# Chosen experts and gates sent to the partitions of their LoRA rows through DRAM instead of by a TensorE product

## The chip, the cores and the metric

One core of one Trainium2 chip. The time is device microseconds of one execution of the whole kernel, the median of several runs. The profile is one further execution, recorded instruction by instruction.

## The reference

One layer on `x` of 128 batches, each 128 nodes by 1024 features, with an integer adjacency matrix for each batch. Cut to what matters:

```python
x = x + gnn(layernorm(x), adj, adj, W, a)          # Wh = h @ W, 16 heads of 64, masked softmax, att @ Wh, elu
y = layernorm(x)
logits = einsum('bh,eh->be', y[:, 0, :], router_w)  # E = 8 experts, from node 0 of the batch
top_vals, top_idx = top_k(logits, 2)                # two experts for each batch
gates = softmax(logits kept at top_idx, -inf elsewhere)
down = einsum('blh,erh->bler', y, lora_down)        # R = 16 rows an expert
x = x + y + einsum('bler,ehr,be->blh', down, lora_up, gates)
```

Each batch so has two chosen experts, of 16 LoRA rows each, and two gates.

## The kernel before

**Passes and gaps.** The batches are taken in 64 pairs, a pass q for each pair (and two passes to run out), and in 32 groups of four (G = 4). A pass of the loop at L835 loads the next pair and projects its own pair with W. The projection is done as seven products in the order 1, 6, 2, 5, 7, 3, 4 (`project`, L390 to 476), each 8 products of 128x128 by 260 columns in the program (L417) and 16 rows in the trace. Ahead of each product stands a list of tasks, a gap: gap 0 before product 1, gap 1 before product 6, gap 2 before product 2, gap 3 before product 5, gap 4 before product 7, gap 5 before product 3, gap 6 before product 4, and gap 7 after it. The order of every engine's instructions is the order in which the program writes them (`manual_schedule`, L71), so the gaps are an order written out by hand: an engine takes its instructions from the gaps one after the other and waits at each for its operands. SP, which issues most DMAs, is such a queue too. Waits between engines are set by the framework from the tiles' reads and writes.

**Where a group's experts are handled.** For group g:

- pass 2g+2, gap 6: `logits` (L609) makes the logits of four batches on PE, `choose` (L620) picks on DVE two experts a batch; `val[:, 0]` holds their numbers (as 8 - e) and `val[:, 1]` later the gates, a batch on each of 4 partitions.
- pass 2g+3, gap 0: `fetch` (L677) stands first, then `attention_weights` (L494) of another pair, then `weigh` (L657), which makes the gates.
- gap 3: `gates` (L696). Gap 4: `ffn_down` (L701), with `pd` (L707) on PE from the fetched rows of `down`, and ACT's multiplication by the gate (L713). Gaps 5 and 6: `ffn_up` (L715), from `up`.

The 128 LoRA rows of a group (4 batches, 2 slots, 16 rows) lie on 128 partitions. So the 8 experts' numbers have to come from 4 partitions to all 128 (`at_down`, L682, eight numbers on each partition, the addresses of eight gathers), and each number to the 16 partitions of its slot (`at_up`, L685, the addresses of one gather). The gates have to come to the partitions of their slot as well (`gate`, used in L713).

Before the change this is done by `spread` (L646) and `to_rows` (L667): DVE multiplies the two numbers of each batch by a row of the identity matrix, which gives 4 partitions by 8 numbers with zeros elsewhere; PE multiplies these by a matrix of ones (`ones_g`) and so puts all eight on every partition of a PSUM tile `pb`; DVE masks them with `slot` and sums, which gives the one number that belongs to each partition. `pb` takes a buffer of the pool `ps_m` (4 of them), as do `ph`, `pd`, `pu` and `pl`.

POOL issues the eight gathers of `down` (L688) and the one of `up` (L692). The last group has no `fetch`; it uses all experts densely.

**SP's queue** around it: in pass 2g+2 the load of `adj_i` (L105) in gap 5; ahead of gap 0 of pass 2g+3 two loads of `xt` (L101) and two of `xn` (L96); then the two transposes by DMA (L586) of gaps 2 and 3; then four stores (L730) in gap 6. `adj_f` (L107) is loaded through POOL's queue.

Of the kernel before, what the change touches and what calls it, by code (L numbers as in the profile page):

```python
# [8 lines left out]
F32 = mybir.dt.float32  # L9
# [5 lines left out]
ALU = mybir.AluOpType  # L15
AX = mybir.AxisListType
# [9 lines left out]
def adj_ffn_kernel(  # L26
# [15 lines left out]
    nc = tc.nc  # L42
    B, N, D = x.shape
    P = 128
# [6 lines left out]
    R = ER // E  # L51
    TOP = 2
    GR = TOP * R
    HALF = 512
# [3 lines left out]
    NG, _, G, _ = adj.shape  # L58
# [5 lines left out]
    const = ctx.enter_context(tc.tile_pool(name="const", bufs=1))  # L64
    work = ctx.enter_context(tc.tile_pool(name="work", bufs=2))
    small = ctx.enter_context(tc.tile_pool(name="small", bufs=3))
    ps_w = ctx.enter_context(tc.tile_pool(name="ps_w", bufs=2, space=bass.MemoryType.PSUM))
    ps_m = ctx.enter_context(tc.tile_pool(name="ps_m", bufs=4, space=bass.MemoryType.PSUM))
# [7 lines left out]
    GRP = {}  # L76


    dram = ctx.enter_context(tc.tile_pool(name="dram", bufs=1, space=bass.MemoryType.DRAM))
# [70 lines left out]
    ident = const.tile([P, P], F32, name="ident")  # L150
# [2 lines left out]
    nc.vector.memset(half_pow, -0.5)  # L153
    fold = small.tile([P, H], F32, tag="fold", name="fold", bufs=1)
    nc.vector.tensor_reduce(fold, ident.rearrange("p (t h) -> p h t", t=KH)[:, 0:H], AX.X, ALU.add)
    ones_g = const.tile([G, P], F32, name="ones_g")
    nc.vector.memset(ones_g, 1.0)

    order = const.tile([G, E], F32, name="order")
    for e in range(E):  # L160
# [118 lines left out]
        return fourths([router_sb[:, k] for k in range(KC)],  # L279
                       [down_sb.rearrange("p e r k -> p k (e r)")[:, k] for k in range(KC)])  # L280

    slot = down_row = up_row = None

    def experts(part):

        nonlocal slot, down_row, up_row
        pr = ps_m.tile([P, HALF], F32, tag="pm", name="pr")
        nc.tensor.matmul(pr[:, 0:E + ER], sum_of, part, start=True, stop=True)
        for t, lo, n in ((router_sb.rearrange("p k e -> p e k"), 0, E),
                         (down_sb.rearrange("p e r k -> p (e r) k"), E, ER)):  # L290
            nc.vector.tensor_tensor(t, t, pr[:, lo:lo + n, None].to_broadcast([P, n, KC]),
                                    ALU.subtract)
        nc.sync.dma_start(table.rearrange("(e p) c -> p e c", p=P),
                          down_sb.rearrange("p e r k -> p e (r k)"))

        slot = const.tile([P, 1, G * TOP], F32, name="slot")
        nc.vector.tensor_reduce(slot[:, 0], ident.rearrange("p (j r) -> p j r", r=R), AX.X,
                                ALU.add)
        rows = work.tile([P, P], I32, tag="hp", name="rows")
        nc.gpsimd.iota(rows, pattern=[[0, G * TOP], [1, R]], base=E * R, channel_multiplier=0)  # L300
        at_r = work.tile([P, P], F32, tag="hp", name="at_r")
        nc.vector.tensor_tensor(at_r, rows, ident, ALU.mult)
        up_row = const.tile([P, 1], F32, name="up_row")
        nc.vector.tensor_reduce(up_row, at_r, AX.X, ALU.add)
        row = small.tile([P, 1], I32, tag="row", name="row", bufs=1)
        nc.gpsimd.iota(row, pattern=[[0, 1]], base=E * P, channel_multiplier=1)
        down_row = const.tile([P, 1], F32, name="down_row")
        nc.vector.tensor_copy(down_row, row)
# [311 lines left out]
    def choose(g):  # L620

        st = GRP[g]
        both = small.tile([G, E + 1], F32, tag="lg", name="lg")
        nc.vector.tensor_copy(both, st["pl"][:G, 0:E + 1])
        lg, dev = both[:, 0:E], both[:, E:E + 1]
        top = small.tile([G, 8], F32, tag="top", name="top")
        nc.vector.max(out=top, in_=lg)

        val = small.tile([G, 2, TOP], F32, tag="val", name="val")
        first = small.tile([G, E], F32, tag="first", name="first")  # L630
        mark = small.tile([G, 2, E], F32, tag="mark", name="mark")
        for s in range(TOP):
            nc.vector.scalar_tensor_tensor(mark[:, s], lg, top[:, s:s + 1], order,
                                           op0=ALU.is_equal, op1=ALU.mult)
            if s:
                nc.vector.tensor_scalar(first, order, val[:, 0, 0:1], None, op0=ALU.is_equal)
                nc.vector.scalar_tensor_tensor(mark[:, s], first, float(-E), mark[:, s],
                                               op0=ALU.mult, op1=ALU.add)
            nc.vector.tensor_reduce(val[:, 0, s:s + 1], mark[:, s], AX.X, ALU.max)
        if g < NG - 1:  # L640
            st["experts"] = spread(val[:, 0], "experts")
        pr = small.tile([G, 2], F32, tag="pr", name="pr")
        nc.vector.tensor_sub(pr[:, 0:1], top[:, 1:2], top[:, 0:1])
        st.update(val=val, pr=pr, dev=dev)

    def spread(val, name):  # L646

        own = small.tile([G, G, TOP], F32, tag=name, name=name)
        nc.vector.tensor_tensor(own, ident[:G, :G, None].to_broadcast([G, G, TOP]),
                                val[:, None, :].to_broadcast([G, G, TOP]), ALU.mult)  # L650
        return own.rearrange("g t s -> g (t s)")

    def ratio(g):
        st = GRP[g]
# [2 lines left out]
    def weigh(g):  # L657

        st = GRP[g]
        gate, pr = st["val"][:, 1], st["pr"]  # L660
        nc.vector.tensor_scalar(gate[:, 0:1], pr[:, 1:2], 1.0, None, op0=ALU.add)
        nc.vector.reciprocal(gate[:, 0:1], gate[:, 0:1])
        nc.vector.tensor_mul(gate[:, 1:2], pr[:, 1:2], gate[:, 0:1])
        if g < NG - 1:
            st["gates"] = spread(gate, "gates")

    def to_rows(own, name):  # L667

        pb = ps_m.tile([P, HALF], F32, tag="pm", name="pb")
        nc.tensor.matmul(pb[:, 0:G * TOP], ones_g, own, start=True, stop=True)  # L670
        mine = small.tile([P, G * TOP], F32, tag="mine", name="mine")
        nc.vector.tensor_tensor(mine, pb[:, 0:G * TOP], slot[:, 0], ALU.mult)
        of_slot = small.tile([P, 1], F32, tag=name, name=name)
        nc.vector.tensor_reduce(of_slot, mine, AX.X, ALU.add)
        return pb, of_slot

    def fetch(g):  # L677

        st = GRP[g]
        pb, mine = to_rows(st["experts"], "of_slot")  # L680
        at_down = small.tile([P, G * TOP], U32, tag="at_down", name="at_down")
        nc.vector.tensor_scalar(at_down, pb[:, 0:G * TOP], float(-P), down_row, op0=ALU.mult,  # L682
                                op1=ALU.add)
        at_up = small.tile([P, 1], U32, tag="at_up", name="at_up")
        nc.vector.tensor_scalar(at_up, mine, float(-R), up_row, op0=ALU.mult, op1=ALU.add)  # L685
        st["down"] = work.tile([P, G * TOP * R, KC], F32, tag="down", name="down", bufs=1)
        for j in range(G * TOP):
            nc.gpsimd.indirect_dma_start(  # L688
                out=st["down"][:, j * R:(j + 1) * R].rearrange("p r k -> p (r k)"), out_offset=None, in_=table,
                in_offset=bass.IndirectOffsetOnAxis(ap=at_down[:, j:j + 1], axis=0))  # L690
        st["up"] = work.tile([P, D], F32, tag="up", name="up", bufs=1)
        nc.gpsimd.indirect_dma_start(  # L692
            out=st["up"], out_offset=None, in_=up_t,
            in_offset=bass.IndirectOffsetOnAxis(ap=at_up[:, 0:1], axis=0))

    def gates(g):  # L696

        st = GRP[g]
        st["gate"] = to_rows(st["gates"], "gate")[1]

    def ffn_down(g):  # L701

# [132 lines left out]
    for q in range(NQ + 2):  # L835
        gaps = [[] for _ in range(8)]
        if q == 0:
            prepare(gaps)
        g, part = divmod(q - 2, 2)
        ffn = 0 <= g < NG  # L840
        if ffn and not part:
            gaps[6] += [(logits, g), (choose, g)]
# [3 lines left out]
        if ffn and not part:  # L846
            gaps[6].append((ratio, g))
            if g == NG - 1:
                gaps[6] += [(down_dense, g, 3, 1), (weigh, g)]
# [27 lines left out]
        if ffn and part and g == NG - 1:  # L877
            gaps[0] += [(gates_dense, g), (up_dense, g)]
        elif ffn and part:
            gaps[0].insert(0, (fetch, g))  # L880
            gaps[0].append((weigh, g))
            gaps[3].insert(0, (gates, g))
            gaps[4].insert(0, (ffn_down, g))
            gaps[5].insert(0, (ffn_up, (g, 0)))
            gaps[6].append((ffn_up, (g, 1)))
# [14 lines left out]
        if q == 1:  # L900
            gaps[0].append((squares_of, 1))
            gaps[5].append(keep("tables", table_parts))
            gaps[7].append(keep("", experts, "tables"))
# [50 lines left out]
```

## Time and profile before

| what | value |
|---|---|
| median of 9 runs | 1948.74 us (1947.38 to 1949.59) |
| the profiled execution | 1948.96 us |
| its span, first to last instruction | 1947.2 us |
| granted TensorE clock, mean over the span | 0.996 of full speed |
| `down` gathers (L688), POOL | 248, 1015 ns each |
| `pw` (L417), PE, lhs xt / lhs s | 4080 and 3072 rows, 386 and 384 ns each |
| DMA traffic | 329.25 MB, 169 GB/s in the mean |

The page gives times in microseconds from the first instruction. PE are TensorE's matmuls, PEld its weight loads, DVE is VectorE, ACT ScalarE, POOL GpSimd, SP the engine that issues DMAs; a q behind a name is that engine's sequencer. "L707" is line 707 of the kernel. A row of the timeline has start, length, engine, line, operation, what is written from what, and, in brackets, how long the engine stood idle before it and what ended that. The mean duration of a matmul row holds the overlap with its neighbour; how long a stretch of PE's queue takes is better read from the chain of waits, where the pieces follow one another without overlap.

### The profile page before, as it was taken

To read this page: it belongs to the slowest core of one execution; us is meant where nothing else is said; L and a number is where in the kernel's file an instruction comes from. 1 tells how busy PE (TensorE), PEld (TensorE's weight loads), DVE (VectorE), ACT (ScalarE), POOL (GpSimd) and SP (SyncE) were. 2 spreads that over 40 slices of the span, in tenths; PEclk is the share of its full clock that TensorE was granted. 3 is DMA by queue.
4 is the path that set the end of the run, shared out by engine and by line. 5 is a ranking of instruction groups with operands and counts; after the bars stand their busy time and mean duration, and the time that the engine had idled before them with its cause. 6 is when DMAs were issued, how large, how long until landed. Compare 5 with 4: busy or idle time off the path is not lost.

```text
span 1947.2 us, 30291 instructions
## 1 busy us (share of the span) xinstructions
PE 1931.5 (99%) x11096; PEld 1574.7 (81%) x11096; DVE 1640.6 (84%) x3477; ACT 1088.1 (56%) x1060; POOL 833.8 (43%) x1135
## 2 busy tenths in 40 slices
PE   9999999999999999999999999999999999999997
PEld 6888888888888888888888888888888888888885
DVE  6888888888888888888888888888888888888886
ACT  3655556556555556555555555565555555555653
POOL 3345433355444355333454433553444553334540
PEclk9999999999999999999999999999999999999998
DMA  7455655665655656556546556556556565565452
GB/s 306 130 185 143 181 172 154 186 177 134 198 175 152 190 152 163 184 158 179 184 130 195 171 151 187 168 147 194 168 163 185 146 173 176 155 187 182 124 167 93
DMA packets 343955, 329.25 MB, mean 169 GB/s; under 512 B 274304, under 2 KB 276352, under 8 KB 343296
## 3 DMA queue, kind: packets, MB, share of 16 engines
q1 hardware_dynamic: 326080, 285.35, 49.9%
q0 software_dynamic: 17008, 40.91, 7.1%
q8 instruction: 88, 1.44, 0.3%
q10 hardware_dynamic: 720, 1.06, 0.1%
q14 instruction: 59, 0.48, 0.1%
HBM read 193.57 MB, written 67.63 MB: 134 GB/s over the span
## 4 chain that ended last, share of the span: by engine, by line
PE 95%; DVE 3%; ACT 1%; DMA 1%; issue 0%; POOL 0%; POOLq 0%; DVEq 0%; ACTq 0%
PE pw L417 79%; PE ph L534 6%; PE pu L723 3%; PE pd L707 3%; PE pb L670 1%; PE pl L614 1%; DMA tt<-halves 1%; PE pu L784 1%; DVE xn L553 0%; DVE hp L544 0%; DVE xn L552 0%; DVE stats L314 0%; ACT halves L584 0%; PE idle L149 0%; ACT y_t L590 0%
## 5 line engine op out<-in xcount | busy, mean ns | idle before, releaser
L417 PE MATMUL pw<-w_sb,xt 128*128 128x260 f32 (+1 forms) x4080 | 944.4, 386 | 0.0
L417 PEld LDWEIGHTS pw<-w_sb,xt 128*128 128x128 f32 x4080 | 764.7, 190 | 144.7 <-issue 27.5
L417 PE MATMUL pw<-w_sb,s 128*128 128x260 f32 (+1 forms) x3072 | 711.1, 384 | 1.9 <-DVE u L425 1.9
L417 PEld LDWEIGHTS pw<-w_sb,s 128*128 128x128 f32 x3072 | 578.1, 190 | 115.7 <-POOL xt L370 15.2
L318 POOL TENSOR_SCALAR rstd<-mv 128x2 f32<-128x2 f32 x126 | 27.6, 219 | 850.6 <-DVE mv L315 845.4
L590 ACT COPY y_t<-tt 128x2048 uint16<-128x2048 uint16 x126 | 313.3, 2505 | 68.8 <-DMA tt<-halves 68.4
L688 POOL DMA_INDIRECT down<-table,at_down x248 | 251.8, 1015 | 162.5 <-DVE e L508 88.8
L314 DVE BATCH_NORM_STATS2 stats<-xn 128x6 f32<-128x512 f32 x504 | 318.8, 674 | 0.1
L584 ACT COPY halves<-xn 128x2048 uint16<-128x2048 uint16 x126 | 239.5, 1901 | 124.6 <-DVE xn L553 79.7
L486 ACT ACTIVATE parts<-wh,rstd 128x512 fp32r<-128x512 f32 x192 | 134.2, 716 | 212.2 <-DVE wh L425 212.2
L551 ACT ACTIVATE ex<-hp 128x1024 f32<-128x1024 f32 x128 | 135.3, 1057 | 177.4 <-DVE hp L544 175.9
L727 DVE SCALAR_TENSOR_TENSOR xn<-pu,rstd,xn 128x512 f32<-128x512 f32 x248 | 169.0, 744 | 21.8 <-PE pu L723 21.8
L544 DVE TENSOR_TENSOR hp<-ph,att 128x512 f32<-128x512 f32 x256 | 161.3, 672 | 10.3 <-PE ph L534 10.0
L553 DVE SCALAR_TENSOR_TENSOR xn<-ex,xn 128x1024 f32<-128x1024 f32 x128 | 156.8, 1225 | 14.2 <-DVE xn L552 0.9
L534 PE MATMUL ph<-parts,adj_f 128*128 128x512 f32 x512 | 164.5, 443 | 1.3 <-ACT parts L486 0.8
L552 DVE SCALAR_TENSOR_TENSOR xn<-hp,xn 128x1024 f32<-128x1024 f32 x128 | 156.8, 1225 | 4.4
L425 DVE TENSOR_TENSOR wh<-pw,u 128x520 f32<-128x520 f32 (+1 forms) x128 | 89.2, 697 | 78.8 <-PE pw L417 75.4
L606 ACT ACTIVATE xn<-xn,off,mul 128x1024 f32<-128x1024 f32 x128 | 151.4, 1232 | 1.5 <-POOL off L571 1.5
L490 DVE SCALAR_TENSOR_TENSOR parts<-wh,rstd,parts 128x512 fp32r<-128x512 f32 x192 | 137.9, 746 | 11.1 <-ACT parts L486 11.1
L534 PEld LDWEIGHTS ph<-parts,adj_f 128*128 128x128 f32 x512 | 96.6, 189 | 20.9 <-ACT parts L486 1.2
L425 DVE TENSOR_TENSOR wh<-pw,p 128x520 f32<-128x520 f32 (+1 forms) x64 | 44.8, 699 | 81.3 <-PE pw L417 81.3
L319 POOL TENSOR_TENSOR rstd<-rstd,half_pow 128x2 f32<-128x2 f32 x126 | 89.9, 714 | 10.5
(156 smaller groups left out, 1486.3 us busy)
## 6 DMA issues: line engine op xcount, KB each, us to landing
xn<-in_x SPq DMA_DIRECT2D x128, 512.0 KB
xt<-in_x_t SPq DMA_DIRECT2D x127, 512.0 KB
out_y<-xn SPq DMA_DIRECT2D x124, 512.0 KB
adj_f<-in_adj_t POOLq DMA_DIRECT2D x32, 256.0 KB
adj_i<-in_adj SPq DMA_DIRECT2D x32, 256.0 KB
down<-table,at_down POOLq DMA_INDIRECT x248
w_sb<-in_w SPq DMA_DIRECT2D x3, 1040.0 KB
wt_sb<-in_w_t SPq DMA_DIRECT2D x1, 2048.0 KB
```

The costliest lines, as they stand in the source:

```text
L314: nc.vector.bn_stats(st[:, h, :], X[i][:, h * HALF:(h + 1) * HALF])
L417: nc.tensor.matmul(dst[:, j, cols], lhs[:, k, :], w_sb[:, rhs, k, j, cols], start=(first and k == 0), stop=(k == KH - 1), skip_group_check ...
L490: nc.vector.scalar_tensor_tensor(in_two(PARTS[q][:, 1, b]), block, rstd, in_two(PARTS[q][:, 0, b].bitcast(F32)), op0=ALU.mult, op1=ALU.sub ...
L534: nc.tensor.matmul(PH[i][h], GRP[g]["adj_f"][:, t, :], PARTS[q][:, s, NH * (i % 2) + h], start=(s == 0), stop=(s == 1))
L544: nc.vector.tensor_tensor(hp[:, h * HALF:(h + 1) * HALF].rearrange("p (h f) -> p h f", f=F), ph.rearrange("p (h f) -> p h f", f=F), att[:, ...
L552: nc.vector.scalar_tensor_tensor(xt, hp, 0.0, xt, op0=ALU.max, op1=ALU.add)
L553: nc.vector.scalar_tensor_tensor(xt, ex, 1.0, xt, op0=ALU.min, op1=ALU.add)
L584: nc.scalar.copy(halves, X[i].bitcast(U16).rearrange("p (d s) -> p s d", s=2))
L590: nc.scalar.copy(y_of(i).bitcast(U16).rearrange("p k (n s) -> p s k n", s=2), TT.pop(i).rearrange("p (s k) n -> p s k n", s=2))
L606: nc.scalar.activation(X[i], X[i], AF.Identity, bias=GRP[g]["off"][:, t:t + 1], scale=GRP[g]["mul"][:, t:t + 1])
L688: nc.gpsimd.indirect_dma_start(out=st["down"][:, j * R:(j + 1) * R].rearrange("p r k -> p (r k)"), out_offset=None, in_=table, in_offset=b ...
L727: nc.vector.scalar_tensor_tensor(y[:, cols], pu[t], st["rstd"][:, t:t + 1], y[:, cols], op0=ALU.mult, op1=ALU.add)
```

## The change

The product by ones is replaced by a write to DRAM and reads from it. `put_away` copies the two numbers of each batch 16 times each on DVE (4 partitions by 32), and SP writes them to 128 consecutive numbers in DRAM. `of_rows` reads them back one to a partition, and `of_group` reads all 128 to every partition (128 x 128, of which each sixteenth number is used). The experts' write and both reads are issued in `choose`; the gates' write and read in `weigh`. The task `gates` in gap 3 goes, as do `spread`, `to_rows`, `ones_g` and `slot`. `at_down` reads SBUF where it read PSUM.

```diff
-    ones_g = const.tile([G, P], F32, name="ones_g")
-    nc.vector.memset(ones_g, 1.0)
...
-        slot = const.tile([P, 1, G * TOP], F32, name="slot")
-        nc.vector.tensor_reduce(slot[:, 0], ident.rearrange("p (j r) -> p j r", r=R), AX.X,
-                                ALU.add)
...
         if g < NG - 1:
-            st["experts"] = spread(val[:, 0], "experts")
+            rows = put_away(val[:, 0], "experts")
+            st["experts"] = of_group(rows, "experts_of"), of_rows(rows, "of_slot")
...
-    def spread(val, name):
-
-        own = small.tile([G, G, TOP], F32, tag=name, name=name)
-        nc.vector.tensor_tensor(own, ident[:G, :G, None].to_broadcast([G, G, TOP]),
-                                val[:, None, :].to_broadcast([G, G, TOP]), ALU.mult)
-        return own.rearrange("g t s -> g (t s)")
+    def put_away(val, name):
+
+        own = small.tile([G, TOP, R], F32, tag="own", name="own", bufs=2)
+        nc.vector.tensor_copy(own, val[:, :, None].to_broadcast([G, TOP, R]))
+        rows = dram.tile([P, 1], F32, tag=name, name=name, bufs=2)
+        nc.sync.dma_start(rows.rearrange("(g r) o -> g (r o)", g=G),
+                          own.rearrange("g s r -> g (s r)"))
+        return rows
+
+    def of_rows(rows, name):
+
+        mine = small.tile([P, 1], F32, tag=name, name=name)
+        nc.sync.dma_start(mine, rows)
+        return mine
+
+    def of_group(rows, name):
+
+        every = small.tile([P, P], F32, tag=name, name=name, bufs=1)
+        nc.sync.dma_start(every, rows.rearrange("r o -> o r").to_broadcast([P, P]))
+        return every.rearrange("p (j r) -> p j r", r=R)[:, :, 0]
...
-            st["gates"] = spread(gate, "gates")
-
-    def to_rows(own, name):
-
-        pb = ps_m.tile([P, HALF], F32, tag="pm", name="pb")
-        nc.tensor.matmul(pb[:, 0:G * TOP], ones_g, own, start=True, stop=True)
-        mine = small.tile([P, G * TOP], F32, tag="mine", name="mine")
-        nc.vector.tensor_tensor(mine, pb[:, 0:G * TOP], slot[:, 0], ALU.mult)
-        of_slot = small.tile([P, 1], F32, tag=name, name=name)
-        nc.vector.tensor_reduce(of_slot, mine, AX.X, ALU.add)
-        return pb, of_slot
+            st["gate"] = of_rows(put_away(gate, "gates"), "gate")
 
     def fetch(g):
 
         st = GRP[g]
-        pb, mine = to_rows(st["experts"], "of_slot")
+        every, mine = st["experts"]
         at_down = small.tile([P, G * TOP], U32, tag="at_down", name="at_down")
-        nc.vector.tensor_scalar(at_down, pb[:, 0:G * TOP], float(-P), down_row, op0=ALU.mult,
+        nc.vector.tensor_scalar(at_down, every, float(-P), down_row, op0=ALU.mult,
...
-    def gates(g):
-
-        st = GRP[g]
-        st["gate"] = to_rows(st["gates"], "gate")[1]
...
-            gaps[3].insert(0, (gates, g))
```

More of the change, by code (lines that the diff above doesn't have):

```diff
@@ L280, in table_parts @@
                        [down_sb.rearrange("p e r k -> p k (e r)")[:, k] for k in range(KC)])
-    slot = down_row = up_row = None
+    down_row = up_row = None
     def experts(part):
-        nonlocal slot, down_row, up_row
+        nonlocal down_row, up_row
         pr = ps_m.tile([P, HALF], F32, tag="pm", name="pr")
```

## The prediction

> **What bounds the kernel now.** I read the page first (busy time, then the chain of work that ended last), then that chain over one group of four batches (880 to 945 us), then the timeline of the same stretch, then the waits, then the DMA packets of the trace one by one.
>
> ```profile
> span 1947.2 us, 30291 instructions
> ...
> PE 1931.5 (99%) x11096; PEld 1574.7 (81%) x11096; DVE 1640.6 (84%) x3477; ACT 1088.1 (56%) x1060; POOL 833.8 (43%) x1135
> ...
> PE 95%; DVE 3%; ACT 1%; DMA 1%; issue 0%; POOL 0%; POOLq 0%; DVEq 0%; ACTq 0%
> ```
>
> PE is never without work and the chain runs through it for 95% of the span. The waits agree: no wait of a matmul or weight load in the steady part exceeds 1.6 us, and the largest that names another engine (POOL L370) sums to 15.2 us. A microsecond taken from PE's queue is a microsecond of the span, as long as nothing that PE waits for becomes late. Next, the chain over one group (start, length, what):
>
> ```profile
> 885.13 0.31 PE pb L670 x2
> 885.45 3.70 PE pw L417 x16
> ...
> 913.19 14.03 PE pw L417 x64
> ...
> 927.75 3.70 PE pw L417 x16
> 931.45 0.31 PE pb L670 x2
> 931.76 3.70 PE pw L417 x16
> ```
>
> The reader is to see two things. The small product pb holds PE for 0.31 us. And the projection product behind it takes 3.70 us, while four in a row take 14.03, or 3.51 each: behind a short product the next one starts 0.19 us worse. The products behind pd, pl and pu are 3.70 or 3.71 too, those behind ph 3.51.
>
> **What the change removes on PE.** Both pb of a group go (62 in all; the instruction lists of the two kernels have 5816 and 5754 matmuls on PE). What stands before and behind each pb is then adjacent: product 4 and product 1 at 931.45, product 2 and product 5 at 944.34. Product 2 and product 5 are adjacent in the other pass of every group already, inside the 14.03. So each pb gives back 0.31 + 0.19 = 0.50 us, a group 1.00 us, and 31 groups 31.1 us at the full digits of 0.502. If only the 0.31 came back it would be 19.4 us.
>
> **What it removes on DVE.** Two `mine` (0.15) and two reductions (0.16) a group: 0.62 us. The copy into `own` takes the place of the spread (0.15 each) at the same size class. DVE is not on the path, it only gets a little more room. The memset and the `slot` reduction at the start are off the chain: nothing.
>
> **What it adds.** Per group five transfers on SP's queue: the experts' write, two reads (64 KB and 512 bytes), the gates' write and read. SP issues in order, so each read holds SP until its write has landed. DVE's at_down now waits for a landing instead of for pb; the attention weights of two batches are queued behind it on DVE, and POOL's eight gathers wait for it.
>
> ```profile
> 925.01 0.33 SPq L105 DMA_DIRECT2D adj_i<-in_adj  x1
> ...
> 929.33 0.15 DVE L649 TENSOR_TENSOR experts<-ident,val 4x8 f32<-4x8 f32 x1
> ...
> 931.49 0.70 DVE L425 TENSOR_TENSOR wh<-pw,u 128x520 f32<-128x520 f32 x1 [0.21 <-PE pw L417]
> 931.52 0.85 SPq L101 DMA_DIRECT2D xt<-in_x_t  x2
> ...
> 932.67 0.22 DVE L682 TENSOR_SCALAR at_down<-pb,down_row 128x8 uint32<-128x8 f32 x1 [0.21 <-DMA adj_f<-in_adj_t]
> 932.81 0.20 DVE L685 TENSOR_SCALAR at_up<-of_slot,up_row 128x1 uint32<-128x1 f32 x1
> ```
>
> Here SP has been free since 925.34 when the experts' numbers are spread (929.33 to 929.48), and the hardware queue is empty: the last packets of adj_i end at 927.28. DVE is busy until 932.19 with L425, which stays. So two chained transfers have from 929.5 to 932.2 for nothing, and to 932.67 before at_down is later than now.
>
> **What a transfer costs** the trace shows only for larger ones. adj_i, 256 KB: first packet 0.98 us after issue, last packet 2.29, landing 2.62 (medians of 30), so 1.31 us apart from its data. The last store to out, a write to DRAM of 256 KB: issued 1935.92, first packet 1936.75, last 1937.58, landed 1937.94, so 1.19 apart from its data. A gather's 4096 bytes an engine (the big read has as many) take about 0.2 us. Lower bound: two at 1.31 without data, landing near 932.2, the small read 0.33 us of SP's issue later, nothing late. Upper bound: each as long as the whole of adj_i, 929.55 + 2.62 + 0.05 + 2.62 + 0.33 = 935.2, at_up 2.4 us late. By the nearest rows: write 1.19 + 0.05, SP's next issue 0.05, read 1.31 + 0.2: landed at 932.35, the small read at 932.7, so at_up about where it is now (932.81). POOL's adj_f (packets 930.85 to 932.21) shares the engines with the read, and nothing here shows a 4-byte row or a write that is read back; I take 0.3 us late and keep -0.2 and 2.4 as ends.
>
> The Trainium skill speaks against this. "DMA: Bandwidth & Descriptors", in "Anatomy of one DMA — SWDGE (gpsimd) path", gives each DMA a fixed cost of about 2.0 us, most of it the receipt of the last write, worst into HBM. By that figure the chain would land at about 933.9, 1.1 us late, and the saving would be some 13 us; this trace's 1.2 to 1.3 us on the hardware queue are below the page's figure, which is fitted to the software queue.
>
> **What is late next, if at_down is late.** Three users:
> - DVE's own chain: PE needs `u` read (940.00 to 940.69) before product 5 (944.58, then 943.6) and ACT's copy of p1 (935.51 to 936.10) before product 2 (940.4): some 3 us of room.
> - SP: `xt` starts at 931.52 now; behind the second read it starts near 931.6. Its first reader is POOL L367, 19 us later. The gates' write goes behind 2 MB of xt and x in the same queue (packets to 939.70), so it lands near 940.1 and the gates' read is issued by 940.5, before the transpose at 942.04; ACT reads the gate at 950.3 (891.13 one period of 59.2 us before). No cost.
> - The gathers, which pd on PE needs:
>
> ```profile
> 942.04 7.78 SPq L586 DMA_TRANSPOSE tt<-halves  x2
> ...
> 942.46 0.95 POOL L688 DMA_INDIRECT down<-table,at_down  x1 [0.30 <-issue]
> ...
> 948.29 1.98 PE L707 MATMUL pd<-y_t,down 128*32 128x128 f32 x63
> ```
>
> The eighth gather is issued just behind the transpose and its packets move only when the transpose's are through (946.05). Over the 31 groups its last packet ends 1.11 to 2.27 us before pd starts (the margin; median 2.02); landing takes 0.33 more. pd is to start 1.00 us earlier, and transpose and gathers move by the lateness d of at_up on DVE. So PE waits max(0, 1.33 + d - margin) a group. Summed over the 31 margins: d = -0.2: 0; 0: 0.6 us; 0.3: 2.2; 0.75: 7.3; 1.1: 17.6; 1.5: 30; 2.4: 58. This is where the gain would go; break-even is d of about 1.5, at_up at 934.3.
>
> **The sum.** 31.1 - 2.2 = 28.9 us off the profiled execution's 1948.96 (span 1947.2 and 1.8 around it): 1920.1. That execution is 0.2 above the median of the nine runs, 1948.74; so **1920 us**.
>
> **Rivals.**
> 1. The forecast: d from -0.2 to 0.75, PE contiguous but for a few pd: 1917.6 to 1925. For it: the empty queue and the 1.2 to 1.3 us rows. 0.58.
> 2. The transfers take nearer 2 us each, d from 0.75 to 1.45: pd waits in every group, 1925 to 1945. For it: short rows and the read-back are not in the trace. 0.15, and 0.05 more for a wash (1945 to 1952).
> 3. Slower: the round trip takes over 5 us, at_up later than 934.3. Each further 0.1 us costs 3.1 us on pd. With two transfers as long as adj_i (d 2.4): 1948.7 + 58 - 31 = 1976. For it: transposes take 4.3 us to land (920.13 to 924.46); against it: those move 512 KB. 0.12.
> 4. The 0.19 does not come back, because it belongs to the weights' change of operand and not to pb: 1929 to 1932. Against it: the 14.03. 0.10.
>
> That the change would leave the products in place is excluded by the lists. Differences under 0.2% (3.9 us) can't be told from none. Faster 0.58 + 0.15 + 0.10 = 0.83, same 0.05, slower 0.12. The range 1916 to 1938 takes in cases 1 and 4 and most of 2, about 0.8.
>
> **What would show it.** In the profile after: no pb line; chain pieces of 7.21 or 7.02 us where products 4 and 1, and 2 and 5, meet; a group period of 58.2 to 58.4 us, not 59.20; at_down between 932.5 and 933.3 on this clock, relative to the logits. Wrong if at_down is idle over 1 us on the landing, if pd's weight load names a gather or a DMA, if a projection product waits for DVE, or if the pieces behind the removed pb stay 3.70.

## The result and the profile after

The changed kernel takes 1955.5 us (10 runs, 1951.8 to 1962.5), the kernel before 1948.8: ratio 1.0037, 95% interval 1.0029 to 1.0045. It is 0.4% slower, where 1.5% faster was forecast.

The page after, busy time and the chain that ended last:

```profile
PE 1911.0 (98%) x10972; PEld 1559.9 (80%) x10972; DVE 1621.1 (83%) x3351; ACT 1081.6 (55%) x1060; POOL 816.9 (42%) x1135
...
PE 72%; DVE 13%; DMA 10%; issue 2%; POOL 2%; ACT 1%; SPq 0%; DVEq 0%; POOLq 0%; ACTq 0%
PE pw L411 61%; DMA of_slot<-experts 5%; PE ph L528 4%; PE pu L717 3%; PE pd L701 3%; DVE hp L538 2%; DVE xn L546 2%; DVE xn L547 2%; POOL down L687 1%; DMA experts<-own 1%; DMA tt<-halves 1%; DMA down<-table,at_down 1%; DVE u L419 1%; DVE parts L484 1%; DVE wh L419 1%
```

PE's busy time fell by 20.5 us (1931.5 to 1911.0), as removed work should make it. But PE's share of the chain fell from 95 to 72%, and 10% now are DMA, with the small read `of_slot` as the largest item. The gain is there and is more than given back by new waits. The list of waits of the kernel after names them (engine and tile, what ended the wait, us in total, times, longest):

```profile
DVE at_down L681 <- DMA experts_of<-experts: 77.3, 31, 3.7
...
DVE at_up L684 <- DMA of_slot<-experts: 44.9, 29, 2.2
```

The list of the kernel before has, for the same instruction:

```profile
DVE at_down L682 <- DMA adj_f<-in_adj_t: 4.4, 19, 0.6
```

(`at_down` does not read `adj_f`; the list names what came last by the profile.) So 4.4 us became 122, which is 3.9 us of standing still a group. The timeline of the kernel after shows it for one group, from the write's issue on SP to the two instructions on DVE that wait:

```profile
936.21 0.27 SPq L646 DMA_DIRECT2D experts<-own  x1
...
937.35 0.33 SPq L659 DMA_DIRECT2D experts_of<-experts  x1
937.74 0.42 SPq L653 DMA_DIRECT2D of_slot<-experts  x1
...
941.47 0.23 DVE L681 TENSOR_SCALAR at_down<-experts_of,down_row 128x8 uint32<-128x8 f32 x1 [2.59 <-DMA experts_of<-experts]
...
942.69 0.21 DVE L684 TENSOR_SCALAR at_up<-of_slot,up_row 128x1 uint32<-128x1 f32 x1 [0.99 <-DMA of_slot<-experts]
```

How the wait reaches PE is seen in the chain over the same group (start, length, what):

```profile
937.74 4.86 DMA of_slot<-experts
...
950.03 0.62 DVE u L419
...
950.70 3.77 PE pw L411 x16
954.47 2.08 PE pd L701 x62
```

The experts' write was issued at 936.21 and the two reads at 937.35 and 937.74; the second landed at 942.60. DVE then runs without a pause to `u`, and product 5 (950.70) starts when `u` has been read. pd behind it takes 2.08 us, where it took 1.92. The list of waits of the kernel after has PE itself waiting for `u`, which the list of the kernel before has once (1.9 us):

```profile
PE pw L411 <- DVE u L419: 15.5, 22, 1.9
```

To see it over all groups, the rows of the trace were laid beside each other, for every group from the copy of the logits on DVE (L624 before). Medians in us; "2 to 5" is the stretch from the start of product 2 to the start of pd, with what stands between, and "pd" the stretch from the start of pd to the start of product 7; both are means over the groups, in us of PE's queue, waits included. "First" says in how many of 30 groups the first transpose is issued ahead of the eighth gather.

| run | time | at_up | transpose | 8th gather | first | 2 to 5 | pd |
|---|---|---|---|---|---|---|---|
| before | 1948.8 | 4.94 | 14.17 | 14.58 | 30 | 7.61 | 1.92 |
| after | 1955.5 | 8.57 | 17.85 | 16.65 | 2 | 8.01 | 2.32 |
| e1 gates only | 1933.2 | 4.94 | 14.17 | 14.58 | 30 | 7.11 | 1.91 |
| e2 experts only | 1953.8 | 8.44 | 17.69 | 16.64 | 1 | 7.89 | 2.23 |
| e3 eight numbers | 2010.1 | 9.63 | 18.89 | 18.17 | 7 | 8.98 | 2.82 |
| e5 small read first | 2040.1 | 9.00 | 18.32 | 18.79 | 30 | 8.31 | 4.65 |
| e6 one short read | 1935.6 | 5.82 | 15.07 | 15.51 | 30 | 7.10 | 2.60 |
| e7 fetch later | 1964.1 | 8.63 | 15.32 | 17.37 | 30 | 7.11 | 3.40 |
| e8 short and later | 1958.3 | 7.84 | 14.42 | 18.04 | 30 | 7.10 | 3.27 |
| e11 big read alone | 1969.7 | 6.80 | 16.03 | 16.44 | 30 | 7.14 | 3.51 |
| e12 short, gates moved | 1922.6 | 5.77 | 16.85 | 15.05 | 1 | 7.10 | 2.06 |
| e13 big, gates moved | 1926.2 | 6.97 | 18.07 | 16.25 | 1 | 7.16 | 2.21 |

The balance of the changed kernel: 0.50 us gained in gap 0; in front of product 5, 7.61 became 8.01 where 7.11 was due, a wait of 0.90; pd 0.40. That is +0.30 a group, 9 us in 31; the spans differ by 8.3.

Not all of pd's 0.40 is a wait for the gathers. In 27 of the 31 groups no row inside pd is held up by more than 0.3 us. What is longer there is the step from pd's last row to product 7, in most of these groups 0.47 us in place of 0.20. Only in four groups does pd itself stand (0.8 to 2.3 us), and in three of these the transpose is issued ahead of the eighth gather (the table leaves out one of the 31).

### The profile page after: what moved, and what is told of

It reads as the page before. It is cut to its first block, busy times and chain, and to the rows that moved or that the text cites. A ratio compares the mean times of both kernels' runs of the same rounds, so it can differ in the third digit from the quotient of the medians.

```text
span 1955.5 us, 30197 instructions
## 1 busy us (share of the span) xinstructions
PE 1911.0 (98%) x10972; PEld 1559.9 (80%) x10972; DVE 1621.1 (83%) x3351; ACT 1081.6 (55%) x1060; POOL 816.9 (42%) x1135
## 4 chain that ended last, share of the span: by engine, by line
PE 72%; DVE 13%; DMA 10%; issue 2%; POOL 2%; ACT 1%; SPq 0%; DVEq 0%; POOLq 0%; ACTq 0%
PE pw L411 61%; DMA of_slot<-experts 5%; PE ph L528 4%; PE pu L717 3%; PE pd L701 3%; DVE hp L538 2%; DVE xn L546 2%; DVE xn L547 2%; POOL down L687 1%; DMA experts<-own 1%; DMA tt<-halves 1%; DMA down<-table,at_down 1%; DVE u L419 1%; DVE parts L484 1%; DVE wh L419 1%
## 5 line engine op out<-in xcount | busy, mean ns | idle before, releaser
L411 PE MATMUL pw<-w_sb,s 128*128 128x260 f32 (+1 forms) x3072 | 712.6, 385 | 21.2 <-DVE u L419 15.5
L419 DVE TENSOR_TENSOR wh<-pw,u 128x520 f32<-128x520 f32 (+1 forms) x128 | 87.7, 685 | 20.5 <-PE pw L411 17.3
L509 ACT ACTIVATE p<-p 128x64 f32<-128x64 f32 x64 | 16.4, 256 | 159.0 <-DVE p L508 88.5
```

Source lines behind the costliest of these rows:

```text
L411: nc.tensor.matmul(dst[:, j, cols], lhs[:, k, :], w_sb[:, rhs, k, j, cols], start=(first and k == 0), stop=(k == KH - 1), skip_group_check ...
L419: nc.vector.tensor_tensor(dst[:, :, cols], src[:, :, cols], plus[:, :, cols], ALU.add)
```

## The experiments

Theory 1 was: the experts' reads land late, DVE stands still for them, and PE waits for what DVE makes. The first rival: what costs is SP's queue, held for landings. Later the question became which of two DMAs the late DVE pushes past the other.

**e1: the gates alone through DRAM.** Edit: the experts' part as before, with `pb` in gap 0.

```diff
-            st["gates"] = spread(gate, "gates")
+            st["gate"] = of_rows(put_away(gate, "gates"), "gate")
...
-            gaps[3].insert(0, (gates, g))
```

> Only the gates go through DRAM; the experts' numbers stay on the product pb. Theory 1 (the experts' reads land 3 us late, DVE's at_down and at_up wait, and product 5 on PE waits for u behind them): the gates' part is free, since ACT needs the gate 10 us later, and the pb in front of product 5 gives back 0.50 us in each of 31 groups: about 1933 us, no idle time in front of product 5. Rival (what costs is SP's queue, held by reads that wait for a write's landing, with transposes and loads behind them): SP is held here too by the gates' write behind 2 MB of loads, so at least part of the loss remains: 1945 us or more.

Measured: 1933.2 us, ratio 0.9916 (0.9900 to 0.9933). The chain over one group:

```profile
921.97 3.70 PE pw L417 x16
925.67 0.31 PE pb L685 x2
...
935.06 7.01 PE pw L417 x32
942.07 1.92 PE pd L717 x64
```

Where the gates' pb stood, products 2 and 5 take 7.01 in one piece instead of 3.51 + 0.31 + 3.70. The gain is 15.5 us against the kernel before run beside it (1948.7), 0.50 for each of 31 pb. The price of a pb and the claim that the gates' two transfers are hidden are both shown, and SP's queue as the cause falls for the gates.

**e2: the experts alone through DRAM.** Edit: `spread` and `to_rows` stay for the gates, the experts go as in the change. Two small temporaries of the attention weights (`m`, `den`) have one buffer, for room, here as in e4, e11, e13 and e14; e4 and e14 show that this costs nothing (1947.3 and 1946.8 us).

> Only the experts' numbers go through DRAM; the gates stay on the product pb in gap 3. (Two small temporaries of the attention weights have one buffer instead of three, for room.) Theory 1: the late at_up is here in full; with pb back, product 5 is due 0.5 us later, so it waits 0.3 to 0.5 us instead of 0.9; gap 0 gives 0.50 back, pd costs up to 0.4 more: 1945 to 1956 us, and at_up about 3 us late as in the changed kernel. Rival (SP's queue): SP is held for the gates no more, so half of the loss goes: about 1938 us.

Measured: 1953.8 us, ratio 1.0025 (1.0015 to 1.0035); at_up at 8.44. The whole loss sits in the experts' half: 1933.2 to 1953.8 stand against each other, with the same number of pb.

**e3: only the eight numbers read by every partition.** Edit: another layout in DRAM.

```diff
-        own = small.tile([G, TOP, R], F32, tag="own", name="own", bufs=2)
+        own = small.tile([G, R, TOP], F32, tag="own", name="own", bufs=2)
...
-        rows = dram.tile([P, 1], F32, tag=name, name=name, bufs=2)
+        rows = dram.tile([R, G * TOP], F32, tag=name, name=name, bufs=2)
...
-        nc.sync.dma_start(every, rows.rearrange("r o -> o r").to_broadcast([P, P]))
+        nc.sync.dma_start(every, rows[0:1].to_broadcast([P, G * TOP]))
```

> As the changed kernel, but the experts' numbers lie in DRAM so that the eight that every partition needs are 32 bytes in a row; the read to all partitions moves 128 x 32 bytes in place of 128 x 512, and the write has 64 pieces of 8 bytes in place of 4 of 128. Theory 1 (the big read's 2.4 us of packets is what is late): the read takes under 0.7 us of packets, at_up comes 1.5 us or more earlier, product 5 waits no more: 1918 to 1930 us. Rival (small reads cost by their number, 128 pieces, whatever their length, or because they follow a write to the same place): at_up as late as before, 1952 to 1958 us.

Measured: 2010.1 us, ratio 1.0299 (1.0270 to 1.0328). The expectation was missed, by the edit itself: the read's packets did fall, from 2.30 to 1.35 us, but the write, now 64 pieces of 8 bytes, kept SP for 3.70 us until its read could be issued, where 4 pieces of 128 bytes take 1.15. at_up came 1.1 us later than in the changed kernel, not earlier.

**e4: the reads without anybody waiting.** Edit, in the kernel before, with the results unused:

```diff
             st["experts"] = spread(val[:, 0], "experts")
+            rows = put_away(val[:, 0], "unused")
+            of_group(rows, "unused_of", g % 3)
+            of_rows(rows, "unused_slot")
```

> The kernel before, with the experts' write, a 64 KB read and the small read added whose results nobody uses; the 64 KB read takes by turns (group modulo 3) the 512 bytes just written for all partitions, 128 different rows of the table, or one row of the table for all partitions. Nobody on DVE waits for them, so this measures the reads alone and SP's holding alone. Theory 1, with one line read 128 times as the cause: packets of the first and the third kind take about 2.4 us, of the second under 1 us; the time stays within 4 us of before. If reading back what was just written is the cause: only the first kind is slow. If the number of pieces is: all three are slow. Rival (SP's queue): the time rises by 5 us or more without any wait of DVE.

Measured: 1947.3 us, ratio 0.9996 (0.9986 to 1.0005). Neither the traffic nor the holding of SP costs anything here, so the price is DVE's wait and what follows it. Packets from first to last, medians: 2.17 us for the line just written, 1.07 for 128 rows, 1.71 for one old row. But the last two do not read what was written and were issued 0.8 us earlier (0.33 us behind the write's issue in place of 1.15), beside adj_f, so e14 repeats it.

**e5: the two reads in the other order.** Edit: `of_rows` is called ahead of `of_group`.

> As the changed kernel, but the 512-byte read (of_slot) is issued ahead of the 64 KB read. Theory (the two reads pass through one queue one after the other, and each is slow by its 128 pieces: 2.3 us and 1.4 us of packets): of_slot lands about 6 us after the logits' copy, the big read at about 8.3 where the small one did, at_down is 1.5 us later than in the changed kernel (6.8) and at_up follows at once; DVE is as late as before, the gathers 1.5 us later: 1955 to 1975 us. Rival (the small read is late only because it stands behind the big one, and alone takes some 1.4 us from issue to landing): of_slot lands at about 4.5, the big read at 7, at_up at about 7.2 in place of 8.6: 1930 to 1945 us.

Measured: 2040.1 us, ratio 1.0457 (1.0440 to 1.0475). The landing behaves as the theory said: the second read decides, at_down comes at 8.86 and at_up at 9.00. The time was missed by 65 us. at_up is hardly later than in the changed kernel, and yet pd takes 4.65 us. So at_up alone does not make the time; pd's wait has a cause of its own. The table has two differences from the changed kernel: the eighth gather comes 2.1 us later, and in all groups behind the transpose.

**e6: one short read.** Edit: the eight numbers are written once and read by one transfer; at_up's number is picked on DVE with `slot`, as before the change.

```diff
+            eight = dram.tile([1, G * TOP], F32, tag="experts", name="experts", bufs=2)
+            nc.sync.dma_start(eight.rearrange("o (g s) -> (o g) s", g=G), val[:, 0])
+            every = small.tile([P, G * TOP], F32, tag="experts_of", name="experts_of", bufs=1)
+            nc.sync.dma_start(every, eight.to_broadcast([P, G * TOP]))
```

> The eight numbers are written once (4 pieces of 8 bytes) and read by one transfer of 128 x 32 bytes; at_up's number is picked from them on DVE with the mask and the sum of the kernel before (0.31 us). The gates go as in the changed kernel. Theory (what is late is the packets of the reads): landing at about 1.65 + 1.15 + 1.25 + 1.35 + 0.3 = 5.7 us after the logits' copy, at_down 0.9 us and at_up 1.2 us later than in the kernel before, product 5 waits no more, pd waits up to 0.6 us a group for the eighth gather behind the transpose: 1922 to 1938 us. Rival (a write of 8-byte pieces is as slow as that of the run with eight numbers, 3.6 us): at_down at about 8.2: 1950 us or more.

Measured: 1935.6 us, ratio 0.9929 (0.9913 to 0.9946). at_down at 5.29, better than reckoned (the read's packets take 0.93 us). Product 5 waits no more. But pd takes 0.69 us a group more than before, 21 us in 31 groups out of the 31 that PE was spared. The write of 4 pieces of 8 bytes takes 1.14 us until its read is issued, so it is not the 8 bytes of a piece alone that made e3's write slow.

**e7 and e8: fetch behind the attention weights.** Edit, on the changed kernel and on e6:

```diff
-            gaps[0].insert(0, (fetch, g))
-            gaps[0].append((weigh, g))
+            gaps[0] += [(fetch, g), (weigh, g)]
```

> As the changed kernel, but fetch (at_down, at_up, the gathers) stands behind the attention weights on DVE instead of in front of them, so that these wait for no landing. Theory (product 5 waits for u because DVE stands still for 3.6 us): DVE reaches at_down at about 7.1 us after the logits' copy and waits for at_up's number until 8.6, u comes about 1 us late in place of 3.6, product 5 waits no more; the gathers start as in the changed kernel or 0.3 us later, and pd waits 0.3 to 0.8 us a group: 1928 to 1945 us. Rival (the gathers' lateness is the price, not DVE's): 1950 us or more.

> The one short read and fetch behind the attention weights together. If DVE's wait is the price, nothing waits for a landing now, and what is left is the gathers' start, 2 to 2.5 us later than in the kernel before: 1920 to 1938 us. If pd's wait for the eighth gather grows with each 0.1 us of lateness as the prediction had it, some 2 us late costs 45 us: about 1963 us.

Measured: 1964.1 us (1.0075, 1.0059 to 1.0092) and 1958.3 us (1.0045, 1.0028 to 1.0062). DVE is no longer held and product 5 no longer waits (7.11 and 7.10), as theory 1 said; and both kernels are slower than theory 1 expected, the first slower than the change itself, because pd now takes 3.40 and 3.27. For e7 that is what the rival said (1950 us or more, for the gathers' lateness). In e8 the second reckoning of the expectation, the one from the prediction, was close, 1963 against 1958, but by luck: it took the gathers to be some 2 us late, and the eighth was 3.46 us late (18.04 in place of 14.58), for which the prediction's formula gives 91 us and not 45. Nor does e8's gather stand behind the transpose: the first transpose's packets end 0.4 us after the gather's issue, and the gather's first packet moves 1.7 us after it, as it does when no transpose is ahead of it. pd waits there because the gather is late by itself. In e7 it is mostly that too: the gather's first packet comes 2.4 us after issue, 0.7 more than with no transpose ahead of it.

**e9 and e10: pd one gap later.** Edit, on e6 and on the changed kernel: ffn_down to gap 5, ffn_up to gaps 6 and 7.

> The one short read, and ffn_down and ffn_up each one gap later (pd in front of product 3, the two pu in front of product 4 and behind it). In the run with the one short read alone pd took 2.60 us in place of 1.91, waiting for the eighth gather; 3.7 us later that gather has landed. Theory (that wait is all that is left of the loss): pd is back at 1.91 us and the time is 1935.6 - 31 x 0.69 = 1914 us, 1912 to 1920. Rival (the sums of pu on DVE, now behind product 4, push the attention weights of the next pass, and product 5 or the products of that pass wait): 1925 us or more.

> The changed kernel with ffn_down and ffn_up one gap later, to part its two waits. Theory (of the 1.2 us a group that PE waits in the changed kernel, 0.9 are product 5's for u behind the held DVE and 0.3 to 0.4 pd's for the gathers): pd is back at 1.91, product 5 waits 0.9 us as before: 1955.5 - 31 x 0.4 = 1943 us, 1938 to 1948. If pd's lateness was the greater part: 1930 us or less. If moving pu costs as much as it gains: 1950 us or more.

Measured: 1974.2 us (1.0128, 1.0111 to 1.0145) and 2083.9 us (1.0701, 1.0679 to 1.0723). pd is at 1.91 in both, so the wait was for the gathers; but the time of e9 fell on the rival's side, by another mechanism than the rival's. The group's y_t can only be overwritten behind pd, ACT's copies move back, and the logits wait for y_t (28.0 us in 31 waits of PE in e9). That is about half of the 60 us between 1914 and 1974; the rest was not traced. In e10 products 2, 5 and 7 with their waits take 14.58 us in place of 10.62; that a DVE 3.5 us late has no room for four more sums of pu would explain it, but was not tried. The two waits of the changed kernel were not parted by this.

**e11: the big read alone.** Edit: e6 with the changed kernel's write and its 64 KB read.

> The changed kernel without the small read: the 64 KB read (128 x 512 bytes of the 512 just written) stays, at_up's number is picked on DVE by mask and sum. (Two small temporaries of the attention weights have one buffer instead of three, for room.) Theory (the small read, behind the big one in the queue, adds 1.8 us to at_up): at_down at 6.4 to 6.8 us after the logits' copy, at_up 0.5 behind it and 1.5 us earlier than in the changed kernel, product 5 waits no more. What pd waits hangs on whether the transpose, 1.4 us earlier too, is issued ahead of the eighth gather: 1925 us if behind it, up to 1955 if ahead. Against the one short read (1935.6) the difference is the big read's packets, 2.3 in place of 0.9 us.

Measured: 1969.7 us, ratio 1.0112 (1.0081 to 1.0143). Without the small read at_up is 1.8 us earlier, product 5 waits no more, and the kernel is 14 us slower than the change. The timeline of one group tells why (start, length, engine):

```profile
954.93 8.66 SPq L583 DMA_TRANSPOSE tt<-halves  x2
...
955.34 0.94 POOL L690 DMA_INDIRECT down<-table,at_down  x1 [0.30 <-issue]
...
959.72 1.94 PE L704 MATMUL pd<-y_t,down 128*32 128x128 f32 x58 [1.66 <-DMA down<-table,at_down]
```

The eighth gather is issued 0.41 us behind the transpose, and pd stands 1.66 us for it. In the changed kernel the order was the other one in 28 of 30 groups, because there DVE's standing still delays the transpose by 3.7 us and the gather, which waits for at_down only, by 2.1.

**e12 and e13: the transpose held back.** Edit, on e6 and on e11: weigh goes from gap 0 to gap 2, in front of `turn`. Nothing on the gathers is touched; SP issues the first transpose behind the landing of the gates' write, 1.8 and 2.0 us later.

```diff
-            gaps[0].append((weigh, g))
...
+            gaps[2].insert(gaps[2].index((turn, 2 * q - 2)) if q < NQ else len(gaps[2]), (weigh, g))
```

> The one short read, and weigh (the gates, their write and read) moved from gap 0 to gap 2, just in front of the first transpose on SP's queue. SP then issues that transpose behind the landing of the gates' write, at about 17.4 us after the logits' copy in place of 15.1, while the eighth gather is issued at 15.4 as before. Theory (pd waits because the eighth gather's packets stand behind the transpose's, not because it is issued late): the gather's packets end 1 us or more before pd is due, pd falls from 2.60 to between 1.91 and 2.2, and the time to 1914 to 1924 us. Rival (the gather is late by itself, or the later transpose makes the copy into y_t and the next logits wait): 1935 us or more.

> The same move of weigh in the run with the big read alone (1969.7 us, pd 3.51 us, transpose at 16.07 and eighth gather at about 16.1). Theory of the order: the transpose goes behind the gather, pd falls to 2.2 to 2.6, and the time by 28 to 40 us, to 1930 to 1942. Rival (lateness of the gathers alone): pd stays above 3 us and the time above 1955.

Measured: 1922.6 us (0.9868, 0.9850 to 0.9885) and 1926.2 us (0.9881, 0.9863 to 0.9899). A group of e13 in the timeline:

```profile
941.40 0.94 POOL L690 DMA_INDIRECT down<-table,at_down  x1 [0.30 <-issue]
...
943.16 7.28 SPq L583 DMA_TRANSPOSE tt<-halves  x2
...
944.81 1.99 PE L704 MATMUL pd<-y_t,down 128*32 128x128 f32 x64
```

The gather goes first, 3.4 us ahead of pd, and pd starts without a wait. From e11 to e13 one task was moved and 43.5 us went. The gather is issued only 0.19 us earlier (16.25 in place of 16.44), at most 6 us in 31 groups; pd's stretch fell by 1.30 us, 40 us in 31. So in e11 pd's wait is the order of transpose and gather. The packets say the same: issued 0.41 us behind the transpose, the gather's first packet moves 3.25 us after its issue (medians of the kernel before, e6 and e11), issued ahead of it 1.66 us (the changed kernel, e12, e13). In e12 the gather also comes 0.46 us earlier than in e6, so there the two are not parted. In one group of e12 and one of e13 the transpose still goes first, and there the stretch of pd takes 6.1 and 9.3 us. e12 is 26 us faster than the kernel before, and its chain has the shape that the prediction described:

```profile
917.77 7.21 PE pw L414 x32
...
930.35 7.01 PE pw L414 x32
937.36 1.92 PE pd L705 x64
```

**e14: three kinds of 64 KB read in the same place.** Edit: e4 with the small read in front.

> The unused reads again, with the small read in front, so that the 64 KB read of all three kinds is issued behind the landing of the write and at the same distance from POOL's load of adj_f. If reading one line 128 times is what costs: the second kind (128 rows) has under 1.2 us of packets, the first and the third over 1.5. If it is reading what was just written: only the first is slow. If it was adj_f beside it: all three alike.

One execution, 1946.8 us. Packets from first to last, medians of about ten each:

| 128 x 512 bytes from | us |
|---|---|
| the line just written | 3.74 |
| 128 rows of the table | 0.60 |
| one row of the table | 3.24 |

The first packet comes 1.1 to 1.2 us after issue in all three, behind the same small read. Reading one line 128 times is what costs. That it was just written adds 0.5 us in the medians here and in e4, within the spread of single groups (1.5 to 5.2 us for the first kind, 2.6 to 4.0 for the third). Both reads of one line are slower here, behind the small read, than in e4 in front of it (2.17 and 1.71); e5, with the same order as here, has 3.99.

## Why the prediction was wrong

- **PE's side held.** 0.50 us for a pb, 0.31 and the 0.19 behind it: e1 gave 15.5 us for 31 of them, and 7.01 and 7.21 stand in e12's chain. Rival 4 is out. Two of the prediction's own signs of being wrong came instead: at_down idle for over 1 us (77.3 us in 31 times), and a projection product that waits for DVE.
- **The gates held.** Their write and read cost nothing (e1), and SP's holding costs nothing (e4).
- **The step that failed is the price of the reads.** "A gather's 4096 bytes an engine (the big read has as many) take about 0.2 us": the big read took 2.30 us of packets, since all its pieces come from one line. (The row was read short as well: 0.2 is one packet of the gather; its 16 take 0.5 us from first to last.) And the small read, reckoned 0.33 us behind the big one, landed so late that at_up starts 1.8 us behind at_down (8.57 and 6.77). The write was right (1.15 us to SP's next issue, 1.24 reckoned). at_up came 3.6 us late; I took 0.3 and gave 2.4 as the upper end, so that even the bound was too low. A row of equal bytes was taken for a row of equal kind: the gather reads 128 different rows, the new read one row 128 times.
- **The path to PE was half right.** The room in front of product 5, "some 3 us", was about right (3.6 late less 0.9 of wait leaves 2.7), and with 3.6 it is used up. The formula for pd was wrong for this kernel: 3.6 us late would have cost over 90 us. It let transpose and gathers move together, but the gathers hang on at_down (+2.0) and the transpose on at_up (+3.6), so their order turned round and pd was spared. Where the order stays (e5, e6, e11), pd's wait is 0.7 to 2.7 us and makes most of the loss. Where the two do move together the formula is short: in e6 both are 0.9 us later, for which it gives 11 to 12 us, and pd cost 21.
- **Rival 3** named the right mechanism for a loss, the landing behind the break-even (at_up 3.6 us late, break-even at 1.5), but put its price on pd, where product 5 waited, and reckoned 1976 us for at_up 2.4 us late. It had 0.12.
- The Trainium skill's 2.0 us fixed cost for a DMA ("DMA: Bandwidth & Descriptors", "Anatomy of one DMA — SWDGE (gpsimd) path") was too much for the write here, on the hardware queue: 1.12 to 1.15 us from issue to the next issue that waited for it. It was too little for the reads: 3.7 us from issue to landing for the big one (median), of which 2.30 are its packets.
- The same page ("Queues, rings and completion order") has each DMA engine go round between its queues packet by packet. The trace does not show the eighth gather taking such turns: before the change, issued at 942.46, it moved its first packet at 945.63, when the transpose's packets (943.26 to 946.03, another queue) were nearly through; the sixth had needed 1.7 us from issue. Whether a row of the trace is a packet in the page's sense, no run here tells, so the rule is not refuted.

**Open.** In most groups of the changed kernel pd takes 2.18 us although the packets of its last gather are through 1.0 us before it starts. The time is lost between pd's last row and product 7, in groups in which product 5 had waited; that PE's sequencer had no time to run ahead after that wait would explain it, but was not tried. Why a read of one line takes longer behind the small read (e5, e14) is open too. Why one line is slow to read 128 times, in the memory or in the DMA engines, no run here tells.

## What to carry to other kernels

A detour through DRAM is free where its reader comes 10 us later (the gates). Where an engine in order stands in front of it (the experts) it costs what it lands too late; here it paid when the landing stayed within the room of product 5 and the gather was kept ahead of the transpose (e12 and e13, 26 and 23 us faster than before). So count the landings in series against the room of whatever is queued behind the waiting instruction. Take the price of a transfer from a row with the same pattern of addresses, not with the same bytes. When a wait moves, ask which DMAs it moves by different amounts: here putting one gather back in front of one transpose was worth some 40 us (e11 to e13), more than the products removed.

## What the hardware showed that was not expected

- 128 reads of one 512-byte line: 3.2 to 3.7 us of packets; 128 reads of different rows, issued at the same point: 0.60 (e14). With no read in front of it, 2.0 to 2.3 us (e11, the changed kernel). With 32 bytes a piece, alone: 0.93 (e6).
- A write of 64 pieces of 8 bytes into one 512-byte line let the read that waited for it be issued 3.7 us after its own issue, one of 4 pieces of 128 bytes 1.15, one of 4 pieces of 8 bytes 1.14 (e3, the changed kernel, e6).
- A gather that is issued 0.4 us behind a DMA transpose moves its first packet when that is nearly through, 3.25 us after issue; ahead of it 1.66 us (e11, e13). The order decides over 1.6 us.
